# Four-bit weight codes unpacked in six vector operations instead of ten, and other orders of the sums and of two layer norms, in a macaron transformer block

## The chip, the cores and the metric

The kernel runs on one core of a Trainium2 chip. A core has a matrix engine (TensorE, "PE" in the profile; its weight loads are "PEld"), a vector engine (VectorE, "DVE"), a scalar engine (ScalarE, "ACT"), a general engine (GpSimd, "POOL") and an engine that here only issues transfers (SyncE, "SP"). Each works through its own instructions in the order in which they were written, and waits on semaphores for the others. The metric is the time of one execution on the device in microseconds. An order of instructions is written out by hand in this kernel: what the Python code calls first is first in its engine's queue.

## What is computed

One sequence of 2048 tokens of 512 numbers goes through half a feed-forward step, attention, and half a feed-forward step:

```python
x = x + 0.5 * ffn(layernorm(x), ...)
x = x + attention(layernorm(x), w_qkv, b_qkv, w_out, b_out)     # 16 heads of 32, causal
x = x + 0.5 * ffn(layernorm(x), ...)                            # the same weights as in the first

def dequant(W_packed, scales):          # two 4-bit codes in an integer, low one first
    idx = stack([W_packed & 15, W_packed >> 4 & 15]).reshape(N, K)
    return LUT[idx] * scales per block of 32
    # LUT = 0, .5, 1, 1.5, 2, 3, 4, 6 and the same with a minus sign
def ffn(x, ...):                        # 512 -> 4096 -> 512
    gate, up = x @ Wg.T, x @ Wu.T
    return (gelu_tanh(gate) * up) @ Wd.T
```

Bit 3 of a code is the sign, bits 2 and 1 an exponent and bit 0 a fraction; the table is that of such a small floating-point number, whose exponent zero is subnormal (0 and 0.5).

## The kernel before

**Phases.** `ffn(1, ...)`, `attention(...)` and `ffn(2, ...)` follow each other (L1035 to L1043). The tokens stay in SBUF as 16 tiles of 128 (`xs`). Phase 1 unpacks the weights and stores them in DRAM (`kept`); phase 2 loads them from there, so unpacking happens in phase 1 alone.

**The feed-forward step.** The 4096 hidden units are taken in 8 groups `g` of two halves `h` of 256. Tokens are taken in two halves `tp` of 1024, each of two blocks `tb` of 512. A product of two 2x2 block matrices is made from seven block products instead of eight (the Winograd scheme), which needs sums of blocks: of weights (`Rows.steps`, on GpSimd, L273 to L276: s3, then the changed a21, then s2, then s4), of tokens (`token_sums`, on VectorE, L295 to L298: t3, the changed b12, t2, t4) and of the hidden values (L399 to L402). Tile names in the profile: `w` weights, `xT_f` normalized and transposed tokens, `xsum` token sums, `pg` and `pu` gate and up products in PSUM.

`slot` (L320) makes the gate and then the up products of one half and one `tp`. The products' numbers run in the order 1, 2, 6, 7, 5, 4, 3. Number 1 is copied from PSUM by ScalarE into `u2` (L354), number 5 into `u4` (L366); the others are added by VectorE as they come (L357, L360, L363, L368, L372, L375), with one sum on GpSimd (L369). A gelu on ScalarE (L335) and a product on VectorE (L339) follow. Product 6 is the first that needs s2 and t2; 7 needs s3 and t3, 5 the changed blocks, and 3 and 4 s4 and t4. PSUM has seven buffers for all of these products and for transposes, taken in turn, so a product waits for the reading of the one seven before it.

After each product `slot` runs `rate` steps of a list `background` (the unpacking and the sums of weights needed later), one group of steps of layer norms in the first slots (`early` and `late`), and one step each of two more lists. The first slots of a phase are (h=0, tp=0), (h=1, tp=0), (h=0, tp=1), (h=1, tp=1) for the first group. The down projection follows each pair of slots (`down_pieces`).

**Unpacking.** `dequant_steps` (L212) works on 128 partitions by 512 words. Ten VectorE operations: shift and mask the magnitudes of both codes into two fp16 halves of a word (L233 to L235), bring the signs into place (L236, L237), turn the magnitude into its value by a multiplication, an addition and a minimum in fp16 (L239, L240), put the sign in (L241), and multiply by the scales once per code (L229, twice). They use three tiles: the codes `pk` (two buffers), `mag` and `val`. The codes and scales are loaded on SP's queue by `load_codes`. Phase 1 does this 48 times: 16 for gate, 16 for up, 16 for down weights.

**Layer norms.** `Norm` gives steps for a block of four tiles: moments (VectorE, `bn_stats` and `bn_aggr`, L112 and L113, or on ScalarE with `moments_on_act`), scales (a root on ScalarE and a reciprocal on VectorE, or with `power=True` a power on GpSimd, L124), a normalization of each tile (ScalarE if its number is in `on_act`, L142, otherwise VectorE, L144), and a transpose of each on TensorE with a copy from PSUM by ScalarE (L150, L151). The method `tiles()` gives n0, n1, t0, n2, t1, n3, t2, t3 (n for normalization, t for transpose).

At the start of phase 1 (L496 to L500) the norms of blocks 0 and 1 are written out ahead of the first slot, together with the unpacking of the first gate and up weights:

```python
n0 = Norm("f1", 0, xT[0], normed)
n1 = Norm("f1", 1, xT[1], normed, on_act=(0, 1), power=True)
gate, up = rows.steps(0), rows.steps(1)
run(n0.steps() + n1.moments + [n1.scales] + gate[:5] + n1.tiles() + gate[5:])
run(token_sums(0) + up)
```

Blocks 2 and 3 are normalized inside the first two slots: moments (ScalarE) and scales (GpSimd) in the first, normalizations and transposes in the second.

**The end of attention.** Heads go in pairs `p`, 0 to 7. For the last pair, `attend` takes two chunks of keys at a time; there are 40 chunks, 24 to 39 for the last 512 queries, of which 30 to 33 lie on the diagonal. For each such pair of chunks TensorE makes scores (L835, L844), ScalarE exponentials (L867), and TensorE the values of an earlier chunk (L774). After each chunk `n`, the steps that `extra` holds for `n` are run; among them is phase 2's first norm, of blocks 0 and 1 (L953 to L959): ten steps each, for block 0 one per chunk from 26 on, for block 1 two per chunk from 33 on. After the chunks come the last divisions (L810 and L813) and output projections (L659, added by VectorE in L662). Then phase 2 begins with `token_sums(0)`.

## Time and profile before

| what | us |
|---|---|
| median of the three runs shown | 3284.56 (3282.46 to 3284.75) |
| profiled execution, its own time | 3284.09 |
| span from first to last instruction in it | 3282.3 |
| TensorE busy (matmuls) | 3239.4 (99%) |
| VectorE busy | 2027.8 (62%) |
| GpSimd busy | 1145.8 (35%) |
| ScalarE busy | 875.7 (27%) |
| first feed-forward product starts | 21.21 |
| phase 2's first product starts | 2113.60 |

The profile is one execution taken by the hardware's profiler. A line of the time-ordered view gives start, duration, engine, source line, operation, what is written from what, and how many instructions were merged; in brackets stands how long the engine had been idle before it and what ended that idle time ("issue": nothing that the profile shows). Matmuls overlap, so a row of them is longer than the distance to the next by the end of the last one. The row of tenths shows the busy share in 40 slices of 82 us. In a table by stretches, each engine's busy time stands with its number of instructions, then the granted TensorE clock, the share of the transfer engines and GB/s.

### The profile page before, as it was taken

The page shows a single profiled execution, that of the slowest core. Times are in us where ns is not written, and L with a number is a line of the kernel's source. Part 1 is how long each engine was busy: PE and PEld are TensorE (multiplying, and loading weights), DVE is VectorE, ACT ScalarE, POOL GpSimd, SP SyncE. Part 2 cuts the span into 40 slices and gives each one's busy share as a digit, 9 for nine tenths or more (in the row PEclk, how much of TensorE's full clock was granted, in tenths as well). Part 3 has the DMA queues.
Part 4 walks back from the last instruction along what each step waited for, and adds up shares of the span by engine and source line. Part 5 has one row for each costly group of instructions (what it writes and reads, how often), then busy time and mean ns, then how long its engine had stood idle before and what let it go on. Part 6 is the DMA issues. An engine that isn't in the chain of part 4 may idle for free.

```text
span 3282.3 us, 34191 instructions
## 1 busy us (share of the span) xinstructions
PE 3239.4 (99%) x12656; PEld 1721.3 (52%) x12656; DVE 2027.8 (62%) x3110; ACT 875.7 (27%) x1849; POOL 1145.8 (35%) x1340
## 2 busy tenths in 40 slices
PE   6999999999999999999999999999999999999999
PEld 3556565655656565333344333356556565655556
DVE  7777777777777655565654675554455455445545
ACT  4111111111111131454543556431111111111111
POOL 3456464645646440332212223113122222313222
PEclk9999999999999999999999999999999999999999
DMA  3111111111111100000000000101010101101101
GB/s 137 47 66 66 68 42 71 65 45 67 67 68 42 74 17 7 6 15 6 13 5 6 30 20 9 49 23 45 23 55 36 45 23 45 37 31 45 45 23 52
DMA packets 42055, 134.15 MB, mean 41 GB/s; under 512 B 5864, under 2 KB 26344, under 8 KB 35360
## 3 DMA queue, kind: packets, MB, share of 16 engines
q1 hardware_dynamic: 41888, 131.96, 11.0%
q8 instruction: 100, 1.64, 0.2%
q14 instruction: 67, 0.55, 0.1%
HBM read 81.91 MB, written 48.46 MB: 40 GB/s over the span
## 4 chain that ended last, share of the span: by engine, by line
PE 94%; ACT 2%; DVE 2%; issue 1%; POOL 1%; DMA 0%; SPq 0%; POOLq 0%; DVEq 0%; ACTq 0%
PE po L414 23%; PE pu L315 23%; PE pg L315 23%; PE av L774 8%; PE pm L709 6%; PE pqk L620 4%; PE ps L835 2%; PE pv L637 2%; PE pp L659 2%; PE ps L844 1%; ACT pt L867 1%; PE pt_f L150 0%; ACT both L783 0%; PE pt_a L150 0%; POOL attnT L813 0%
## 5 line engine op out<-in xcount | busy, mean ns | idle before, releaser
L414 PE MATMUL po<-wd,inter 128*128 128x256 f32 x2048 | 482.2, 379 | 0.0
L315 PE MATMUL pg<-xT_f,w 128*128 128x512 f32 x1024 | 475.9, 592 | 2.2 <-DVE w L229 1.5
L315 PE MATMUL pu<-xT_f,w 128*128 128x512 f32 x1024 | 476.1, 592 | 1.3 <-DVE c L368 1.3
L414 PEld LDWEIGHTS po<-wd,inter 128*128 128x128 f32 x2048 | 389.0, 190 | 155.2 <-issue 106.0
L724 DVE TENSOR_REDUCE parts<-pm 128x1 f32<-128x512 f32 (+3 forms) x640 | 370.6, 608 | 149.6 <-PE pm L709 135.5
L369 POOL TENSOR_TENSOR u<-u,u 128x512 f32<-128x512 f32 x128 | 163.4, 1277 | 846.2 <-ACT u L366 846.2
L428 POOL TENSOR_TENSOR x<-x,d 128x512 f32<-128x512 f32 x248 | 333.3, 1355 | 343.6 <-DVE x L422 173.2
L315 PE MATMUL pg<-xsum,w 128*128 128x512 f32 x768 | 359.3, 597 | 3.9 <-issue 2.0
L414 PE MATMUL po<-wd,s 128*128 128x256 f32 x1536 | 362.4, 379 | 0.0
L315 PE MATMUL pu<-xsum,w 128*128 128x512 f32 x768 | 355.4, 592 | 0.4 <-DVE u L372 0.4
L414 PEld LDWEIGHTS po<-wd,s 128*128 128x128 f32 x1536 | 291.4, 190 | 116.2 <-issue 79.6
L709 PE MATMUL pm<-kT,qT 32*128 32x512 f32 (+3 forms) x1280 | 334.2, 574 | 0.1
L867 ACT ACTIVATE pt<-ps 128x512 f32<-128x512 f32 (+3 forms) x576 | 271.7, 532 | 132.8 <-PE ps L844 131.4
L774 PE MATMUL av<-pt,vaug 128*64 128x512 f32 (+3 forms) x1280 | 300.0, 553 | 2.8 <-ACT both L783 2.3
L315 PEld LDWEIGHTS pg<-xT_f,w 128*128 128x128 f32 x1024 | 194.3, 190 | 195.1 <-issue 179.5
L315 PEld LDWEIGHTS pu<-xT_f,w 128*128 128x128 f32 x1024 | 194.2, 190 | 193.4 <-issue 180.8
L844 PE MATMUL ps<-qT,kT 32*128 32x512 f32 (+3 forms) x1280 | 278.9, 536 | 0.0
L315 PEld LDWEIGHTS pg<-xsum,w 128*128 128x128 f32 x768 | 146.4, 192 | 148.1 <-issue 136.9
L315 PEld LDWEIGHTS pu<-xsum,w 128*128 128x128 f32 x768 | 145.7, 190 | 145.1 <-issue 136.8
L422 DVE SCALAR_TENSOR_TENSOR x<-po,x 128x512 f32<-128x512 f32 x192 | 131.5, 685 | 112.8 <-ACT d L436 83.2
L861 POOL TENSOR_SCALAR_AFFINE_SELECT pt<-pt 128x256 f32<-128x256 f32 x128 | 52.3, 408 | 395.9 <-ACT pt L860 394.7
L422 DVE SCALAR_TENSOR_TENSOR d<-po,d 128x512 f32<-128x512 f32 x192 | 131.8, 686 | 82.1 <-PE po L414 81.2
(140 smaller groups left out, 3606.2 us busy)
## 6 DMA issues: line engine op xcount, KB each, us to landing
kept<-wd SPq DMA_DIRECT2D x8, 1792.0 KB
wd<-kept SPq DMA_DIRECT2D x8, 1792.0 KB
x<-in_x SPq DMA_DIRECT2D x16, 256.0 KB
pk<-in_gate_codes SPq DMA_DIRECT2D x16, 256.0 KB
sc<-in_gate_scales SPq DMA_DIRECT2D x32, 128.0 KB
pk<-in_up_codes SPq DMA_DIRECT2D x16, 256.0 KB
sc<-in_up_scales SPq DMA_DIRECT2D x32, 128.0 KB
pk<-in_down_codes SPq DMA_DIRECT2D x16, 256.0 KB
```

The source lines that it names most:

```text
L315: nc.tensor.matmul(ps, lhsT=a[:, j, :], rhs=b[:, j, :], start=(j == 0), stop=(j == 1))
L369: nc.gpsimd.tensor_tensor(u4, u4, u2, ALU.add)
L414: nc.tensor.matmul(ps[:, j, :], lhsT=a[i][:, k, bass.ts(2 * q + j, P)], rhs=b[i][:, k, :], start=(k == 0), stop=(k == 1),)
L422: stt(dst, ps, 0.5, other, ALU.mult, ALU.add)
L428: adder.tensor_tensor(dst, dst, other, ALU.add)
L620: nc.tensor.matmul(ps, lhsT=w[:, j, k, :], rhs=xT[tb][:, k, :], start=(k == 0), stop=(k == 3))
L637: nc.tensor.matmul(ps[:, i, :], lhsT=xT[t // 4][:, k, (t % 4) * P : (t % 4 + 1) * P], rhs=wv_sb[:, k, bass.ts(half, 256)], start=(k == 0), ...
L709: nc.tensor.matmul(ps[a][:, :n], lhsT=q[r, bass.ts(4 * g + i, P)], rhs=k[r, kb * 512 : kb * 512 + n], start=True, stop=not on_pe,)
L724: nc.vector.tensor_reduce(parts[:, a, i, kb : kb + 1], ps[a][:, :n], AX.X, ALU.max)
L774: nc.tensor.matmul(av[64 * a : 64 * a + 64, off:], lhsT=vaug[:, c, p % 4, HD * a : HD * a + 2 * HD], rhs=pt[:, a, off:], start=(c == 0), s ...
L844: nc.tensor.matmul(ps[a][:, off:], lhsT=k[r, bass.ts(c, P)], rhs=q[r, g * 512 + off : (g + 1) * 512], start=False, stop=True,)
L867: nc.scalar.activation(pt[:, a, plain:], ps[a][:, plain:], AF.Exp, scale=scale)
```

## The change

Six things are changed.

- The unpacking takes six operations: the signs and both codes are brought into the two halves of a word in place, the three magnitude bits are shifted to bits 9 to 11 of each half, and sign and magnitude are joined. Such a half, read as fp16, has the code's exponent as its two lowest exponent bits and the code's fraction as its highest fraction bit; it is the code's value divided by 16384, and subnormal for 0.5. The scaling multiplies by 16384 instead of 0.25. The result lies in the codes' tile itself, so `val` is gone and `pk` is held until the second scaling.
- The weights' sums: s2 is made second, as a22 - s3, ahead of the changed a21.
- The token sums: t2 is made second, as t3 + b11, ahead of the changed b12. In phase 2, for the first half of the tokens, t3 is made on GpSimd.
- The tile `u2` has two buffers instead of one.
- The first norms: block 1 takes its scales by a root on ScalarE and a reciprocal on VectorE, its tiles 0 and 1 are normalized on GpSimd and 2 and 3 on VectorE, into tiles of their own tags (`u3`, `c11`), and are transposed in the order 2, 0, 3, 1. Two operations of the unpacking come ahead of block 1's scales and four after its normalizations.
- The last pair's norm of block 1: its ten steps come after chunks 32, 33, 34, 35, 36, 36, 37, 37, 38, 39 instead of two per chunk from 33 to 37.

```diff
+        def __init__(
+            self, phase, tb, t_out, temp, on_act=(0, 1, 2, 3), on_pool=(), moments_on_act=False, power=False
+        ):
...
-                    nc.vector.tensor_scalar(xn[i], tiles[i], mv[:, i, 0:1], rstd[:, i : i + 1], ALU.subtract, ALU.mult)
+                    eng = nc.gpsimd if i in on_pool else nc.vector
+                    eng.tensor_scalar(xn[i], tiles[i], mv[:, i, 0:1], rstd[:, i : i + 1], ALU.subtract, ALU.mult)
...
-                val = dq.tile([P, 512, 2], F16, tag="val", name=f"val_{nm}")
+                val = pk.bitcast(F16).rearrange("p (n b) -> p n b", b=2)
...
-                    stt(o, v, 0.25, s, ALU.mult, ALU.mult)
+                    stt(o, v, 16384.0, s, ALU.mult, ALU.mult)
...
-                    lambda: tsc(mag, w, 9, 0x0E00, ALU.logical_shift_left, ALU.bitwise_and),
-                    lambda: stt(mag, w, 21, mag, ALU.logical_shift_left, ALU.bitwise_or),
-                    lambda: tsc(mag, mag, 0x0E000E00, 0x40004000, ALU.bitwise_and, ALU.bitwise_or),
-                    lambda: tsc(v32, w, 12, 0x8000, ALU.logical_shift_left, ALU.bitwise_and),
-                    lambda: stt(w, w, 24, v32, ALU.logical_shift_left, ALU.bitwise_or),
-
-                    lambda: tsc(v16, f16, 2.0, -4.0, ALU.mult, ALU.add),
-                    lambda: nc.vector.tensor_tensor(v16, f16, v16, ALU.min),
-                    lambda: stt(v32, w, 0x80008000, v32, ALU.bitwise_and, ALU.bitwise_or),
+                    lambda: tsc(mag, w, 12, 0xF000, ALU.logical_shift_left, ALU.bitwise_and),
+                    lambda: stt(w, w, 24, mag, ALU.logical_shift_left, ALU.bitwise_or),
+                    lambda: tsc(mag, w, 3, 0x0E000E00, ALU.logical_shift_right, ALU.bitwise_and),
+                    lambda: stt(w, w, 0x80008000, mag, ALU.bitwise_and, ALU.bitwise_or),
                     lambda: scaled(0),
                     lambda: scaled(1),
...
                         lambda: eng.tensor_tensor(s3, a11, a21, ALU.subtract),
+                        lambda: eng.tensor_tensor(s2, a22, s3, ALU.subtract),
                         lambda: eng.tensor_tensor(a21, a21, a22, ALU.add),
-                        lambda: eng.tensor_tensor(s2, a21, a11, ALU.subtract),
...
+                first = nc.gpsimd if phase == 2 and tp == 0 else eng
...
-                    lambda: eng.tensor_tensor(t3, b22, b12, ALU.subtract),
+                    lambda: first.tensor_tensor(t3, b22, b12, ALU.subtract),
+                    lambda: eng.tensor_tensor(t2, t3, b11, ALU.add),
                     lambda: eng.tensor_tensor(b12, b12, b11, ALU.subtract),
-                    lambda: eng.tensor_tensor(t2, b22, b12, ALU.subtract),
...
-                            u2 = temp("u2", 1)
+                            u2 = temp("u2")
...
+                tags = ["u3", "u3", "c11", "c11"]
                 n0 = Norm("f1", 0, xT[0], normed)
-                n1 = Norm("f1", 1, xT[1], normed, on_act=(0, 1), power=True)
+                n1 = Norm(
+                    "f1", 1, xT[1], lambda nm: ap.tile([P, D], F32, tag=tags.pop(), name=nm, bufs=2),
+                    on_act=(), on_pool=(0, 1),
+                )
                 gate, up = rows.steps(0), rows.steps(1)
-                run(n0.steps() + n1.moments + [n1.scales] + gate[:5] + n1.tiles() + gate[5:])
+                tiles = n0.tiles()
+                run(n0.moments + [n0.scales] + n1.moments + tiles[:6] + gate[:2] + [n1.scales] + tiles[6:])
+                run([n1.normal[i] for i in (0, 2, 1, 3)] + [n1.transposed[i] for i in (2, 0, 3, 1)] + gate[2:])
...
-                            extra.setdefault(STARTS[3] + (2 + i if tb == 0 else 9 + i // 2), []).append(step)
+                            after = 2 + i if tb == 0 else (8, 9, 10, 11, 12, 12, 13, 13, 14, 15)[i]
+                            extra.setdefault(STARTS[3] + after, []).append(step)
```

More of the change, by code (lines that the diff above doesn't have):

```diff
@@ L78, in macaron_kernel @@
     class Norm:
-        def __init__(self, phase, tb, t_out, temp, on_act=(0, 1, 2, 3), moments_on_act=False, power=False):
+        def __init__(
+            self, phase, tb, t_out, temp, on_act=(0, 1, 2, 3), on_pool=(), moments_on_act=False, power=False
+        ):
             nm = f"{phase}_{tb}"
@@ L216, in dequant_steps @@
                 mag = dq.tile([P, 512], U32, tag="mag", name=f"mag_{nm}")
-                val = dq.tile([P, 512, 2], F16, tag="val", name=f"val_{nm}")
-                f16 = mag.bitcast(F16)
-                v16 = val.rearrange("p n b -> p (n b)")
-                v32 = v16.bitcast(U32)
+                val = pk.bitcast(F16).rearrange("p (n b) -> p n b", b=2)
                 tsc, stt = nc.vector.tensor_scalar, nc.vector.scalar_tensor_tensor
```

## The prediction

> **What bounds the kernel.** I read the page's busy times and slices first, then the chain that ended last, TensorE's waits, a table by stretches cut where those waits lie, and the instructions in order of time around them.
>
> ```profile
> PE 3239.4 (99%) x12656; PEld 1721.3 (52%) x12656; DVE 2027.8 (62%) x3110; ACT 875.7 (27%) x1849; POOL 1145.8 (35%) x1340
> PE   6999999999999999999999999999999999999999
> ...
> PE 94%; ACT 2%; DVE 2%; issue 1%; POOL 1%; DMA 0%; SPq 0%; POOLq 0%; DVEq 0%; ACTq 0%
> ```
>
> TensorE is busy everywhere but in the first slice (82 us). The change removes no matmul, so it can gain only where TensorE waits. Columns of the next table: stretch, its length, then busy us of PE, PEld, DVE, ACT, POOL, granted clock.
>
> ```profile
> 0.00:21.21 21.21, 7.99 (x33) 6.10 (x33) 12.79 (x30) 10.72 (x17) 3.40 (x12) 1.00 0.79 247
> 21.21:50.57 29.36, 25.07 (x56) 10.27 (x56) 24.41 (x34) 13.59 (x35) 15.82 (x16) 1.00 0.32 117
> 50.57:78.08 27.51, 20.33 (x53) 10.06 (x54) 18.77 (x30) 13.11 (x25) 8.47 (x10) 0.75 0.22 86
> 78.08:91.35 13.27, 13.23 (x39) 6.19 (x38) 10.40 (x15) 4.66 (x8) 1.53 (x1) 1.00 0.11 40
> ```
>
> A product of two 256-deep matmuls takes 1.72 us (28 instructions in 12.02 us), 14 products a slot, 24.0 us. The first slot takes 29.36. The gate half of the second (12.0 plus six tiles' transposes at 0.5) takes 27.5, partly at half clock. After 78.08 nothing is lost until the last head pair. The places:
>
> ```profile
> 20.37 1.29 DVE L229 SCALAR_TENSOR_TENSOR w<-val,sc 128x512 f32<-128x512 f16 x2
> 21.21 3.67 PE L315 MATMUL pg<-xT_f,w 128*128 128x512 f32 x8 [1.51 <-DVE w L229]
> ...
> 26.77 3.70 PE L315 MATMUL pg<-xsum,w 128*128 128x512 f32 x8 [1.89 <-POOL w L275]
> ...
> 56.80 0.59 ACT L354 COPY u<-pg 128x512 f32<-128x512 f32 x1 [2.98 <-POOL u L369]
> 58.15 1.13 PE L150 MATMUL pt_f<-ident,xn_f 128*128 128x128 f32 x4 [3.88 <-ACT xn_f L142]
> 65.42 1.13 PE L150 MATMUL pt_f<-ident,xn_f 128*128 128x128 f32 x4 [2.72 <-ACT xn_f L142]
> ...
> 2090.75 0.72 PE L150 MATMUL pt_f<-ident,xn_f 128*128 128x128 f32 x4 [2.82 <-DVE xn_f L144]
> 2119.18 3.67 PE L315 MATMUL pg<-xsum,w 128*128 128x512 f32 x8 [1.98 <-issue]
> ```
>
> The first weights are ready at 21; the third product waits for a sum on GpSimd; the second slot waits for normalized tiles; the last pair does too; phase 2's third product waits for its token sum (L297 ends 2119.07, hence "issue" at 2119.18).
>
> **The skill.** "VectorE: DVE Perf Modes", the tier table, has a one-input operation in SBUF at twice the rate of a two-input one; the trace agrees: 0.42 us (L235) against 0.69 (L234). "SBUF — State Buffer", Who interferes with whom: VectorE's two-input and two-port operations contend with GpSimd; the same token sum takes 1.22 us alone and 1.63 beside GpSimd. "TensorE: Matmul & The Clock Gate", Part 1: an idle window of about 3.4 us halves the clock, and Part 4 says that transposes don't count as work. Here the clock is 0.50 from 58 to 70 us after the 3.88 us wait, and 0.50 from 2091.4 to 2094.6 after the 2.82.
>
> **The change, part by part.**
>
> *Start of phase 1.* VectorE's order to 11.85 us (moments of both norms) stays. Then come two unpacking operations (0.43 + 0.73, start to start), done at 13.0. The second norm's root now goes to ScalarE behind the fourth normalization (ends 13.34): 0.30 (no table load lies between the first root and the normalizations), reciprocal 0.18, so scales at 13.85. Before, the power on GpSimd was done at 14.88 and VectorE stood still from 14.5 to 17.15. Two tiles on VectorE at 0.55 end at 14.95, or 15.5 if GpSimd holds the port. GpSimd's one-input pass over 512 elements has no row: affine_select on 256 took 0.41, a two-input sum on 512 1.27; I take 0.9 each (range 0.65 to 1.3), done at about 15.7, or 16.5 at worst. TensorE has four tiles from 14.5, done by 17; ScalarE's copies end about 17.6. VectorE's remaining four operations: 15.5 + 0.43 + 0.73 + 2 x 0.63 = 17.9, the first half of the weights at 17.3. **First product 17.4 instead of 21.21.**
>
> GpSimd now makes s3, then s2: two sums (1.1 and 1.6, partly contended) from 17.9, done 20.6, not third in line (26.71 before). VectorE's token sums start at 17.7; t2 is second, 17.7 + 2 x 1.6 = 20.9. The third product wants to start at 17.4 + 3.67 = 21.1: **no wait, 21.1 instead of 26.77.** The up half then starts at 21.1 + 5 x 1.72 = 29.7 (was 35.45). Its weights: token sums end 24.0, six operations 0.43 + 0.72 + 0.43 + 0.72 + 2 x 0.63 = 3.6, ready at 27.6, against 34.15 before.
>
> *First two slots.* Everything ScalarE and VectorE do next hangs on that 27.6. Before, the next evacuation (L357) started 1.4 us after 34.15, and ScalarE's gelu, sums, squares and copy ran to 43.0; moved 6.5 us they end at 36.5. TensorE's twelfth product then waits about 0.5 for a bank (before: 1.30 and 0.39), and the second slot's first product waits 1.2 for the copy behind the second set of sums (43.6): **slot two at 43.65 instead of 50.57.** The squares end at 46.4, two copies at 47.5. The second of these (L354) waited until 56.80 for GpSimd because its tile had one buffer; with two it doesn't. Normalization 0.82: first transpose at 48.4 after a wait of 1.3 (was 3.88). The next needs ScalarE past the gelu of c11, which waits for VectorE: L369 on GpSimd ends at 49.6 behind the norm's scales; two VectorE operations and one unpacking (1.7) bring 51.3; c11, gelu, normalization 0.7 + 0.6 + 0.8: 53.45, a wait of 2.85 (was 2.72). I take the clock as staying full, since the idle time between products is 1.8 and 3.35 us, not the 4.8 of before. From 53.45: 4 products, 5 tiles at 0.47 and a wait of 0.6 give **the up half at 63.3 instead of 78.08: 14.8 us.** From there the trace has no wait, and I add none.
>
> *Other unpackings.* Four operations fewer in each of 46 more calls, in effect those of L234, L235, L239 and L240. From 92 to 1160 us these are busy 47.2 + 20.9 + 44.7 + 35.9 = 148.7 us in 43 calls, 3.5 a call. All of it is covered by TensorE: group 3's gate weights are scaled by 424.2 and first used at 452.55, its up weights by 448.9 and 476.65, 28 us of cover. Without cover each call would be worth 3.5. The codes' buffer is now held to the second scaling, 5 us longer at 419 to 424; the next load on SP is behind a scales' load that waits for this anyway, and its data are used at 454.
>
> *Last pair's norm.* Its first moments move one step ahead, under VectorE's wait for the transpose (idle 3.91 us before 2084.83); the transposes move to the next two pairs of chunks. From 2087.93 TensorE goes on with scores. Gone are 2.82, 0.25, and half of the 3.2 us at half clock, 1.6: **4.7 us.** Two tiles' copies come later, but before the copy that the divisions hang on, so that chain moves as a whole.
>
> *Phase 2's token sums.* The first goes to GpSimd behind L813 (ends 2112.58): 1024 elements at the slope of 0.72 (256) and 1.27 (512) are 2.4, done 2115.0, as VectorE comes free (2115.34); t2 is then first there and ends at 2116.6, before the third product (2117.2). **2.0 us.** If contended to 4 us, 1.0 would be left.
>
> Sum: 14.8 + 4.7 + 2.0 = 21.5. Span 3282.3 - 21.5 = 3260.8; the profiled execution took 3284.09, 1.8 more than its span, and lies within 0.5 of the median: **3262.6 us.**
>
> **Rivals.** (a) The waits of 1.3 and 2.85 in slot two still halve the clock: 3 to 5 us given back, about 3267; for it, 2.82 was enough in the last pair. 0.18. (b) The last pair gains nothing, as scores wait for banks that ScalarE frees (it has 2 us of exponentials per pair): 3267. 0.10; with (a), 3270 to 3272, 0.04. (c) VectorE runs so far ahead that slot two's waits go too, 5.9 us more: 3257. 0.11. (d) Slower: the scaling reads subnormal fp16, an operand that no row shows. It takes 0.63 alone and up to 1.36 on average. The same skill page, Specifications, says that VectorE computes in fp32, where these numbers are normal, so I take no extra cost; the lower bound is none too, as the other 4 bytes are the same. It makes VectorE the bound only if each takes some 4.8 us more: from 92 to 1160 us VectorE is idle 262 us (1068.0 less 806.0 busy), the removed operations give 149, shared by 86 scalings: (262 + 149) / 86 = 4.8. 0.05. (e) No measurable change, the waits having merely moved: 0.02.
>
> **Numbers.** The forecast as worked has 0.50 (own range 3260 to 3266). 3256.5 to 3271 takes in (a), (b), (c) and the bounds of GpSimd's passes. Slower than 0.2% (6.6 us, about what a measurement can tell) is (d); faster is the rest, 0.93.
>
> **What would show it.** Right: first product near 17.4, third without a wait on GpSimd, slot two near 43.7, its up half near 63, no wait of L150 near 2087, and none before phase 2's third product. Wrong: half clock between 45 and 60 us, GpSimd's normalization above 1.3 us, or new waits after 92 us.

## The result, and the profile after

The changed kernel takes 3267.42 us (median of four, 3266.87 to 3267.80), where the kernel before, measured beside it, takes 3283.51: a ratio of 0.9951, 95% interval 0.9934 to 0.9968. That is 16.1 us gained where 21.5 were forecast. The profiled execution took 3267.61 us, 1.8 more than its span of 3265.8, as before.

The profile of one execution is shown here, as for the kernel before. The busy times and slices of its page, in the columns of before:

```profile
PE 3236.0 (99%) x12656; PEld 1720.2 (53%) x12656; DVE 1887.5 (58%) x2918; ACT 873.4 (27%) x1848; POOL 1130.4 (35%) x1339
PE   7999999999999999999999999999999999999999
```

VectorE lost 140 us of work, and TensorE's time is what it was: the first slice alone looks different, 7 tenths instead of 6. The table by stretches, cut at the same four events (first product, slot two, its up half, 13.27 us of undisturbed work after it):

```profile
0.00:19.86 19.86, 8.09 (x32) 6.26 (x33) 11.55 (x27) 8.79 (x15) 7.14 (x12) 1.00 0.88 279
19.86:46.43 26.57, 26.17 (x57) 11.17 (x56) 20.86 (x29) 14.21 (x36) 14.46 (x17) 1.00 0.35 121
46.43:68.48 22.05, 17.43 (x52) 8.74 (x53) 14.14 (x22) 12.89 (x25) 6.20 (x8) 0.92 0.27 106
68.48:81.75 13.27, 13.23 (x38) 6.20 (x37) 9.87 (x15) 4.65 (x8) 1.80 (x1) 1.00 0.10 35
```

The first stretch is 1.35 us shorter than before, the second 2.8, the third 5.5 (22.05 beside 27.51), and the fourth is the same 13.27. The instructions in order of time that answer to those shown of before:

```profile
13.34 1.37 DVE L147 TENSOR_SCALAR xn_f<-x,mv_f,rstd_f 128x512 f32<-128x512 f32 x2
13.41 5.47 POOL L147 TENSOR_SCALAR xn_f<-x,mv_f,rstd_f 128x512 f32<-128x512 f32 x2 [12.04 <-DMA sc<-in_up_scales]
15.81 1.29 DVE L229 SCALAR_TENSOR_TENSOR w<-pk,sc 128x512 f32<-128x512 f16 x2
18.94 1.12 PE L153 MATMUL pt_f<-ident,xn_f 128*128 128x128 f32 x4 [1.14 <-POOL xn_f L147]
19.86 5.57 PE L313 MATMUL pg<-xT_f,w 128*128 128x512 f32 x8
25.27 3.60 PE L313 MATMUL pg<-xsum,w 128*128 128x512 f32 x8
...
46.43 3.70 PE L313 MATMUL pg<-xT_f,w 128*128 128x512 f32 x8 [0.40 <-ACT u L352]
50.93 0.74 PE L153 MATMUL pt_f<-ident,xn_f 128*128 128x128 f32 x4 [0.79 <-ACT xn_f L144]
56.64 0.75 PE L153 MATMUL pt_f<-ident,xn_f 128*128 128x128 f32 x4 [3.25 <-ACT xn_f L144]
57.22 2.88 PE L313 MATMUL pg<-xsum,w 128*128 128x512 f32 x4
...
2098.41 2.36 POOL L293 TENSOR_TENSOR xsum<-xT_f 128x1024 f32<-128x1024 f32 x1
2099.34 3.60 PE L313 MATMUL pg<-xT_f,w 128*128 128x512 f32 x8
2102.78 3.60 PE L313 MATMUL pg<-xsum,w 128*128 128x512 f32 x8
```

The weights are scaled by 17.1, but the last tile comes from GpSimd at 18.9, so the first product starts at 19.86. It and the start of the second run at about half rate (the row of both, eight instructions, takes 5.57 us instead of 3.7). The third product has lost its wait for GpSimd. Slot two still waits twice for normalized tiles, and the longer wait is followed by four instructions in 2.88 us instead of 1.88, at a granted clock of 0.50 from 58 to 61 us. At the end of attention no wait for a tile is left, and phase 2's third product follows the second without a gap.

| place | before | forecast | after |
|---|---|---|---|
| first product | 21.21 | 17.4 | 19.86 |
| phase 1's up half | 35.45 | 29.7 | 33.85 |
| slot two | 50.57 | 43.65 | 46.43 |
| slot two's up half | 78.08 | 63.3 | 68.48 |
| gained there | | 14.8 | 9.6 |
| gained by the last pair | | 4.7 | 4.5 |
| gained by phase 2's token sums | | 2.0 | 2.1 |

The last two rows: scores at one and the same place start at 2081.75 before and 2072.02 after (9.73 earlier), phase 2's first product at 2113.60 and 2099.34 (14.26, so 4.5 more), its third at 2119.18 and 2102.78 (16.4, so 2.1 more). What is missing is all in the first 70 us.

Two things limit how finely single profiles can be read there. The third token tile's statistics begin at 6.28 us before and at 5.85 after, and from 5.34 to 6.83 in the profiles below, ahead of anything that an edit touches, so a place can differ by up to 1.5 us without a cause in the edit; 0.43 of the 9.6 gained at the up half are of this kind. And the profile taken for GpSimd's operations below is of this same kernel up to its last microseconds. In it the first transposes start 0.1 us earlier than in the profile above, the first product at 19.20 and slot two at 45.77, and the second tile is waited for just as long:

```profile
55.98 0.75 PE L153 MATMUL pt_f<-ident,xn_f 128*128 128x128 f32 x4 [3.25 <-ACT xn_f L144]
56.57 1.88 PE L313 MATMUL pg<-xsum,w 128*128 128x512 f32 x4
```

The four instructions behind that wait take 1.88 us here, at a granted clock of 1.00, and the up half starts at 66.17, which is 11.9 us earlier than before instead of 9.6. From the second tile's transpose to the up half it is 10.19 us here and 11.84 above: the half clock cost 1.65 us in one execution of this kernel and nothing in another.

### The profile page after: what moved, and what is told of

The parts are those of the page before. It is cut to its first block, busy times and chain, and to the rows that moved or that the text cites. A ratio compares the mean times of both kernels' runs of the same rounds, so it can differ in the third digit from the quotient of the medians.

```text
span 3265.8 us, 34006 instructions
## 1 busy us (share of the span) xinstructions
PE 3236.0 (99%) x12656; PEld 1720.2 (53%) x12656; DVE 1887.5 (58%) x2918; ACT 873.4 (27%) x1848; POOL 1130.4 (35%) x1339
## 4 chain that ended last, share of the span: by engine, by line
PE 95%; ACT 2%; DVE 1%; POOL 1%; issue 1%; DMA 0%; SPq 0%; POOLq 0%; DVEq 0%; ACTq 0%
PE po L412 24%; PE pu L313 23%; PE pg L313 23%; PE av L779 8%; PE pm L714 6%; PE pqk L625 4%; PE ps L840 2%; PE pv L642 2%; PE pp L664 2%; PE ps L849 1%; ACT pt L872 1%; PE pt_f L153 0%; ACT both L788 0%; DVE parts L729 0%; PE pt_a L153 0%
## 5 line engine op out<-in xcount | busy, mean ns | idle before, releaser
L426 POOL TENSOR_TENSOR x<-x,d 128x512 f32<-128x512 f32 x248 | 323.5, 1315 | 333.2 <-DVE d L420 164.8
```

The source lines that it names most:

```text
L426: adder.tensor_tensor(dst, dst, other, ALU.add)
```

## The experiments

**What was to be told apart.** My theory after the result: the loss is the price of one operation, GpSimd's normalization, which I had guessed at 0.9 us and which took 5.47 for two; without it the start would be as forecast and so would the rest. The rival: the start's gain is lost again in slot two whatever the start does, since something behind it (ScalarE's moments, VectorE's evacuations, the clock) sets its own pace there. Beside that, each part of the change was to get its own price. In all fences below the lines are those of the view in order of time, unless said otherwise.

### Block 1 normalized on VectorE alone

```diff
-                    on_act=(), on_pool=(0, 1),
+                    on_act=(), on_pool=(),
```

> The changed kernel with block 1's tiles 0 and 1 normalized on VectorE instead of GpSimd (about 0.55 us each instead of 3.13 and 2.35). Theory G: GpSimd's two passes, done at 18.9 us, hold the start; then the last transpose comes near 17, the first product near 17.3 instead of 19.86, and the kernel is 2.5 to 4 us faster than the changed one. Rival H: the start is set by ScalarE's copies and the half-rate TensorE; then less than 1 us is gained.

Measured 3266.33 us (3266.18 to 3267.36; ratio to before 0.9950, 0.9935 to 0.9965), so 1.1 less than the changed kernel by the medians, or 0.5 more gained when each is set against the kernel before as measured beside it (16.6 beside 16.1), with intervals that overlap. 2.5 to 4 were expected.

```profile
17.76 3.72 PE L313 MATMUL pg<-xT_f,w 128*128 128x512 f32 x8
22.03 3.67 PE L313 MATMUL pg<-xsum,w 128*128 128x512 f32 x8 [0.55 <-DVE xsum L294]
45.04 3.70 PE L313 MATMUL pg<-xT_f,w 128*128 128x512 f32 x8 [1.67 <-ACT u L352]
55.25 1.01 PE L153 MATMUL pt_f<-ident,xn_f 128*128 128x128 f32 x4 [3.25 <-ACT xn_f L144]
```

The first product is where the forecast had it (17.76 for 17.4), the third comes 3.2 us earlier than in the changed kernel (22.03 for 25.27). Four normalizations on VectorE take 1.91 us in all. But of the 3.2 us only 1.4 are left at slot two: its first product now waits 1.67 instead of 0.40, for ScalarE's copy. The two waits there are the same 0.79 and 3.25, again with half clock behind the second. So both theories hold a part: the price at the start is real, and slot two takes more than half of it back. Even with VectorE alone, slot two is 1.4 us later than forecast (45.04 for 43.65): block 1's transposes end at 18 instead of 17, and the token sums and the third product follow some 0.9 us late.

### GpSimd's operations measured by themselves

The kernel is the changed one, with instructions on scratch added at its very end; 512 and 256 elements, three of each kind. VectorE's last sums run until 3260.66, so the first two passes are beside them, and all the others are alone.

```diff
+    for n in (512, 256):
...
+            nc.gpsimd.tensor_scalar(pc[:, :n], pa[:, :n], pb[:, 0:1], pb[:, 1:2], ALU.subtract, ALU.mult)
...
+            nc.gpsimd.tensor_scalar(pc[:, :n], pa[:, :n], 2.0, 3.0, ALU.subtract, ALU.mult)
...
+            nc.gpsimd.tensor_scalar(pc[:, :n], pa[:, :n], pb[:, 0:1], None, ALU.subtract)
...
+            nc.gpsimd.tensor_tensor(pc[:, :n], pa[:, :n], pb[:, :n], ALU.subtract)
```

> The changed kernel with GpSimd instructions on a scratch tile appended at its end, when the other engines are done: tensor_scalar on 512 and 256 numbers with two per-partition scalars, with two constants, with one per-partition scalar, and tensor_tensor. If the form with per-partition scalars is dear in itself, it takes 2.2 to 2.5 us for 512 alone, against 0.6 to 1.3 with constants; if the 2.35 and 3.13 us at the start came from sharing the port with VectorE, it takes below 1.3 alone. It says nothing on the total time, which grows by the appended work.

The time was 3293.86 us, which holds the added work. First the third instruction of the normalization's kind (two scalars per partition), which is alone, then groups by line and shape, with busy us and mean ns of one after the bar: two constants, one scalar, two tensors.

```profile
3261.29 2.07 POOL L1056 TENSOR_SCALAR probe<-probe 128x512 f32<-128x512 f32 x1
```

```profile
L1058 POOL TENSOR_SCALAR probe<-probe 128x512 f32<-128x512 f32 x2 | 3.8, 1922 | 0.2
L1060 POOL TENSOR_SCALAR probe<-probe 128x512 f32<-128x512 f32 x3 | 4.7, 1561 | 0.3
L1062 POOL TENSOR_TENSOR probe<-probe 128x512 f32<-128x512 f32 x3 | 3.8, 1262 | 0.2
```

The expectation had two branches and missed with both: alone the pass is below 2.2 us, and two constants cost nearly as much as two scalars per partition, so it isn't these scalars that make it dear. The normalization's pass costs 2.07 us alone, 3.8 times VectorE's 0.55 and 1.6 times a two-input sum on the same engine. "GPSIMD Engine Reference", 4.1 Engine selection, calls one-input work there roughly line-rate and two-input work about twice as slow as on VectorE. The second agrees (1.26 against 0.69); the first does not hold for this operation, and the measurement decides. Beside VectorE, at the start, the two passes took 2.35 and 3.13 us (2.34 and 2.57 in this second profile): up to 1.06 more than alone. The probe shows more of this by chance. Beside its second pass VectorE made two two-input sums, and the pass took 3.10 us; beside its first VectorE made one, the pass took 2.09, and the sum 1.06 instead of 0.69. So either side can be the one that is held up.

### Ten operations in the changed kernel

The old unpacking with its `val` tile, and `u2` with one buffer, since both don't fit.

```diff
-                    stt(o, v, 16384.0, s, ALU.mult, ALU.mult)
+                    stt(o, v, 0.25, s, ALU.mult, ALU.mult)
...
+                    lambda: tsc(v16, f16, 2.0, -4.0, ALU.mult, ALU.add),
+                    lambda: nc.vector.tensor_tensor(v16, f16, v16, ALU.min),
...
-                            u2 = temp("u2")
+                            u2 = temp("u2", 1)
```

> The changed kernel with the ten old unpacking operations, and u2 with one buffer (the third tile needs its space; the run u2_one separates that). If the unpacking carries the gain at the start: the first gate weights are still hidden behind GpSimd's normalization, but the first up weights come 2.2 us later, and slot one's evacuations lag again; the second slot's up half moves from 68.5 to 72 to 77 us, 4 to 8 us slower than the changed kernel. Rival: the other orders carry it, and this run is within 2 us of u2_one.

### One buffer for u2 in the changed kernel

```diff
-                            u2 = temp("u2")
+                            u2 = temp("u2", 1)
```

> The changed kernel with one buffer for u2. The second slot's first copy on ScalarE waits again for GpSimd's sum (ends near 52.4 us), so the first tile's transpose comes at 53.9 instead of 50.9; the next one, at 56.6, does not move. If that is all, nothing is lost; but TensorE then stands without a product from 50 to 54.3 us, so the half clock comes earlier and lasts longer: 1 to 3 us slower than the changed kernel. Rival: no difference beyond 0.5 us.

Ten operations: 3275.48 us (3274.80 to 3277.67; ratio 0.9977, 0.9968 to 0.9986). One buffer: 3266.58 us (3265.22 to 3270.90; ratio 0.9952, 0.9937 to 0.9967), no different from two buffers at 3267.42. So the shorter unpacking is worth 8.9 us between these two, which were measured side by side. First ten operations, then one buffer:

```profile
42.99 1.96 PE L321 MATMUL pu<-xT_f,w 128*128 128x512 f32 x4 [1.34 <-DVE c L374]
57.54 1.13 PE L153 MATMUL pt_f<-ident,xn_f 128*128 128x128 f32 x4 [3.88 <-ACT xn_f L144]
65.29 0.75 PE L153 MATMUL pt_f<-ident,xn_f 128*128 128x128 f32 x4 [3.21 <-ACT xn_f L144]
```

```profile
53.02 0.75 PE L153 MATMUL pt_f<-ident,xn_f 128*128 128x128 f32 x4 [3.65 <-ACT xn_f L144]
53.60 1.88 PE L313 MATMUL pg<-xsum,w 128*128 128x512 f32 x4
55.87 0.75 PE L153 MATMUL pt_f<-ident,xn_f 128*128 128x128 f32 x4 [0.39 <-ACT xn_f L144]
```

With ten operations the products wait for VectorE's evacuations again (1.34), both long waits of slot two are back, and its up half starts at 77.16, about 1 us before the 78.08 of the kernel before: without the shorter unpacking the new order at the start brings next to nothing. With one buffer the first tile is late (3.65) and the second is not (0.39); with two it is the other way round, 0.79 and 3.25. The second buffer moves the wait from one tile to the next. With one, the first tile's normalization stands behind a copy that waits 2.75 us for GpSimd's sum; the second one's stands behind a gelu that waits for VectorE either way, and ScalarE reaches it at 55.02 with one buffer and at 55.78 with two. No half clock follows the 3.65 here, and the up half starts at 66.06, as in the second profile of the changed kernel (66.17).

### The end of attention undone

```diff
-                first = nc.gpsimd if phase == 2 and tp == 0 else eng
+                first = eng
...
-                            after = 2 + i if tb == 0 else (8, 9, 10, 11, 12, 12, 13, 13, 14, 15)[i]
+                            after = 2 + i if tb == 0 else 9 + i // 2
```

> The changed kernel with the old places of the last pair's norm steps and with phase 2's first token sum on VectorE (t2 still second). From the last pair's wait at the 1.9 us (2072.0 in the changed kernel) to phase 2's first product: 27.3 us in the changed kernel, 31.9 here, with half clock again. The third product of phase 2 then waits about 0.5 us for t2 rather than 2.0, since the order alone brings most of that gain. Rival: the last pair's gain came from the earlier moments or from elsewhere and the distance stays below 29 us.

One run: 3274.34 us, 6.9 more than the changed kernel's median; it gains 8.6 on the kernel before as measured beside it, where the changed kernel gains 16.1.

```profile
2080.79 1.10 PE L153 MATMUL pt_f<-ident,xn_f 128*128 128x128 f32 x4 [2.82 <-DVE xn_f L147]
2109.39 3.67 PE L313 MATMUL pg<-xsum,w 128*128 128x512 f32 x8 [0.42 <-PE pg L313]
```

The wait of 2.82 is back to the hundredth, and the half clock with it. From the scores at 2072 to phase 2's third product this kernel is 6.6 us later than the changed one (2109.39 beside 2102.78, from starts that lie within 0.3). Some 1.7 of that are more than in the kernel before, since the stretch at half clock lasted longer: eight products of values took 3.54 us in it, where before they took 2.50. Of the wait before that product only 0.42 of 1.98 is back, as the order of the sums (t2 second) is still the new one: the order brings 1.6, and GpSimd's t3 the last 0.4.

### The six operations alone, in the kernel before

```diff
-                    lambda: tsc(v16, f16, 2.0, -4.0, ALU.mult, ALU.add),
...
+                    lambda: stt(w, w, 0x80008000, mag, ALU.bitwise_and, ALU.bitwise_or),
```

> The kernel before with the six-operation unpacking and nothing else. If the unpacking carries the start's gain, phase 2's first product comes 7 to 9 us earlier than before and the time is near 3275; if it needs the other orders (the third product waiting for the third sum on GpSimd, the norm's power on GpSimd), the gain is below 4 us, above 3279. The last pair's wait of 2.8 us and the half clock stay in both.

3277.09 us (3272.62 to 3279.30 in nine runs; ratio 0.9975, 0.9965 to 0.9985): 6.4 us gained.

```profile
24.95 5.37 PE L307 MATMUL pg<-xsum,w 128*128 128x512 f32 x8 [2.32 <-DVE xsum L289]
2073.86 3.25 PE L766 MATMUL av<-pt,vaug 128*64 128x512 f32 x8
2112.11 3.67 PE L307 MATMUL pg<-xsum,w 128*128 128x512 f32 x8 [1.99 <-issue]
```

The first product starts at 19.02, earlier than in the changed kernel, and slot two's up half at 69.00, 9.1 us earlier than before. That is nearly the whole 9.6 that the changed kernel gains there, with GpSimd's pass, the orders of the sums and the second buffer absent. The waits of the end are all there (1.99). Not all of the 9.1 lasts: 8.6 are left at the last pair's scores (2073.16 for 2081.75), and right behind these eight products of values take 3.25 us instead of 1.72, at a granted clock of 0.50, after a wait of 1.88 that the kernel before has too. That is why the profiled run has 7.1 of it at phase 2's third product, and its time, the median of the nine, 6.4.

### The old orders of the sums

The kernel with block 1 on VectorE, and s2 and t2 back in their old places; t3 stays on GpSimd in phase 2.

```diff
-                        lambda: eng.tensor_tensor(s2, a22, s3, ALU.subtract),
...
+                        lambda: eng.tensor_tensor(s2, a21, a11, ALU.subtract),
...
-                    lambda: eng.tensor_tensor(t2, t3, b11, ALU.add),
...
+                    lambda: eng.tensor_tensor(t2, b22, b12, ALU.subtract),
```

> The run norm_vector with the old order of the weights' and the tokens' sums (the changed blocks second, s2 and t2 third from them). In phase 1 the third product waits for t2 as third token sum: it starts 1.2 to 1.7 us later than the 22.03 of norm_vector; but slot two's first product hardly moves, as it waits for ScalarE by 1.67 us in norm_vector. In phase 2, where t3 stays on GpSimd, t2 is second on VectorE and the third product waits about 0.5 us. In all 0 to 2 us slower than norm_vector. Rival: the order of sums carries 3 us or more, as the forecast's arithmetic for the third product has it (26.77 to 21.1).

One run: 3269.52 us. The third product waits 1.96 for t2 and then runs slowly:

```profile
23.67 5.37 PE L313 MATMUL pg<-xsum,w 128*128 128x512 f32 x8 [1.96 <-DVE xsum L295]
```

Yet slot two's up half starts at 67.21, against 67.11 with the new orders (counted from each profile's first transposes it is no later either). In phase 1 the orders of the sums remove a visible wait and no time: slot two absorbs it. The 3.2 us that this run has over the kernel with the new orders come later: by 0.8 before the last pair's scores at 2071, by 1.6 right behind them, where eight products of values take 3.22 us instead of 1.72, and by 0.9 at phase 2's third product, which waits 0.73. Only the last has to do with the edit. The slow products are the clock: 0.51 is granted there, and 1.00 over the same products with the new orders. The wait ahead of them is 1.88 or 1.89 us in all thirteen profiles of this document; four of them have the clock at 0.50 to 0.57 behind it (this one, the six operations alone, and the two kernels with spread moments below), the other nine don't. Kernels with either order are on both sides, so it doesn't follow the orders. The 0.8 stays unexplained.

### The moments of block 3, then of both blocks, moved to VectorE

In the kernel with block 1 on VectorE, phase 1's moments of block 3, and in a second kernel those of block 2 too, are made by VectorE. This tests the reading of the 1.67 above, that ScalarE's moments hold slot two.

```diff
-                Norm(f"f{phase}", tb, xT[tb], normed, moments_on_act=True, power=True) for tb in (2, 3)
+                Norm(f"f{phase}", tb, xT[tb], normed, moments_on_act=phase == 2 or tb == 2, power=True) for tb in (2, 3)
```

> The run norm_vector with the moments of the fourth block in phase 1 taken on VectorE (four times 0.66 + 0.18 us) instead of ScalarE (eight passes, 5.7 us with their readings). Theory A: what is still lost in slot two is set by ScalarE, whose sums and squares stand ahead of the copies and the gelu; then slot two starts without its 1.67 us wait, near 43.4 us, the 3.25 us wait for the second tile shrinks below 1, no half clock follows, and slot two's up half comes at 60 to 63 instead of 67.1: 4 to 7 us faster than norm_vector. Rival V: VectorE's own evacuations set it, and 3.4 us more on VectorE make it slower.

> As vector_moments, with the third block's moments on VectorE too. If ScalarE was the bound, the first evacuations no longer wait for it at 37 us either (2.94 us idle on VectorE there), and it is as fast as vector_moments or up to 1 us faster; if VectorE is the bound by now, it is 1 to 3 us slower than vector_moments.

3268.01 us (3267.70 to 3268.86; ratio 0.9950, 0.9936 to 0.9965) and 3268.07 (3267.98 to 3269.15; 0.9950, 0.9934 to 0.9967): no gain over the kernel with block 1 on VectorE, rather about 1 us less (15.5 and 15.4 gained on the kernel before as measured beside them, where that one gains 16.6). In the first of them:

```profile
55.37 0.63 ACT L333 ACTIVATE c<-c 128x512 f32<-128x512 f32 x1 [8.42 <-DVE c L355]
56.76 1.13 PE L153 MATMUL pt_f<-ident,xn_f 128*128 128x128 f32 x4 [5.61 <-ACT xn_f L144]
```

Slot two starts 1.4 us earlier, at 43.68, and without a wait for ScalarE. Then ScalarE stands idle for 8.42 us until VectorE, which now has the moments too, has evacuated the product that the gelu needs; the normalization is queued behind that gelu, and the wait grows from 3.25 to 5.61. That reading fell: with less on ScalarE and more on VectorE the wait grows, so it isn't the moments' amount on ScalarE that makes the long wait, but VectorE's evacuations.

### The moments spread earlier, and a normalization put ahead of the gelu

What makes VectorE late? Its instructions in the changed kernel, and ScalarE's gelu behind them:

```profile
38.54 0.69 DVE L366 TENSOR_TENSOR c<-pg,u 128x512 f32<-128x512 f32 x1 [2.94 <-ACT u L364]
46.41 0.69 DVE L355 TENSOR_TENSOR c<-pu,u 128x512 f32<-128x512 f32 x1 [1.47 <-ACT u L352]
54.53 0.68 DVE L355 TENSOR_TENSOR c<-pg,u 128x512 f32<-128x512 f32 x1
55.25 0.63 ACT L333 ACTIVATE c<-c 128x512 f32<-128x512 f32 x1 [4.38 <-DVE c L355]
55.78 0.80 ACT L144 ACTIVATE xn_f<-x,nbias_f,rstd_f 128x512 f32<-128x512 f32 x1
```

VectorE stands still 2.94 and 1.47 us for copies that ScalarE makes behind whole groups of moments (four squares, four sums, some 3 us each), and then works without a pause of more than 0.5 us to 54.53, late by that. The gelu waits for it, and the normalization for the gelu. So the two engines seem to hold each other up in turn. Two kernels test it, both with block 1 on VectorE. The first starts ScalarE's moments sooner and spreads them over other products; the second also puts the second normalization of slot two one step earlier, ahead of the gelu.

```diff
+            if phase == 1:
+                early = [n2.moments, [], [n3.moments[0]], [], [n3.moments[1]], [n2.scales], [], [n3.scales]]
```

> The run norm_vector with phase 1's ScalarE moments placed earlier, none moved to another engine: block 2's right behind the first product's copy (ScalarE stood idle there 8.7 us), block 3's behind products 3 and 5. Theory I, the two engines hold each other up: VectorE's evacuations stood idle 2.94 and 1.47 us for ScalarE's copies and are then late in slot two. Without these idles the second slot starts without its 1.67 us wait, near 43.4, the first evacuation of slot two (53.14 in norm_vector) comes near 48.7, the wait for the second tile falls from 3.25 to about 1.8, no half clock follows, and the up half comes near 61.3 instead of 67.1: 5 to 6 us faster than norm_vector. Rival V, VectorE's own work is the bound: the idles go but it is late all the same, and less than 2 us is gained.

```diff
+            if phase == 1:
+                late[0].append(late[1].pop(0))
```

> As moments_early, and in phase 1 the second tile's normalization stands behind the first one's, ahead of the gelu that waits for VectorE. Then the second tile's transpose no longer waits for VectorE, and the up half of slot two comes at 58.5 to 60.5: 1 to 3 us faster than moments_early. If another wait takes its place (the third tile's normalization stands behind the same gelu), below 1 us.

The first: 3263.30 us (3260.49 to 3264.16; ratio 0.9939, 0.9924 to 0.9954). The second: **3259.66 us** (3258.81 to 3260.99; ratio 0.9929, 0.9912 to 0.9945), and the fastest of all. Against the kernel before as measured beside each, the first gains 19.4 us and the second 23.0, where the changed kernel gains 16.1 and the one with block 1 on VectorE 16.6. First the one, then the other:

```profile
45.24 0.63 PE L153 MATMUL pt_f<-ident,xn_f 128*128 128x128 f32 x4
48.88 0.68 DVE L355 TENSOR_TENSOR c<-pg,u 128x512 f32<-128x512 f32 x1
50.99 1.13 PE L153 MATMUL pt_f<-ident,xn_f 128*128 128x128 f32 x4 [3.40 <-ACT xn_f L144]
51.91 3.03 PE L313 MATMUL pg<-xsum,w 128*128 128x512 f32 x4
```

```profile
48.22 0.63 PE L153 MATMUL pt_f<-ident,xn_f 128*128 128x128 f32 x4
49.84 0.63 ACT L333 ACTIVATE c<-c 128x512 f32<-128x512 f32 x1 [3.27 <-DVE c L355]
51.71 0.75 PE L153 MATMUL pt_f<-ident,xn_f 128*128 128x128 f32 x4 [1.14 <-ACT xn_f L144]
```

With the moments spread, slot two starts at 41.80 without a wait, and VectorE's two pauses before it are gone. But 3.0 us are gained where 5 to 6 were expected, for the wait for the second tile is still there (3.40, half clock behind it). The first tile's transpose comes at 45.24 instead of 49.54 and the evacuation that the gelu needs at 48.88 instead of 53.14: TensorE and VectorE are both 4.3 us earlier, so the distance between them, which makes the wait, stays. From 28.28 to 51.10 VectorE is now busy for 22.1 of 22.8 us; what stands ahead of that evacuation is its own work. The up half starts at 62.66, for 67.11 with block 1 on VectorE. With the normalization ahead of the gelu that transpose follows at once (48.22); the gelu still waits 3.27 for VectorE, but what is queued behind it is now the third tile, and TensorE waits 1.14 for that, with no half clock. The up half starts at 59.70, 8.8 us before the changed kernel's. So two things are shown. ScalarE's moments in front of copies that VectorE needs held back the start of slot two, TensorE and VectorE alike, and not the wait inside it. And VectorE's lateness reached TensorE through the gelu in front of the normalization. How short the wait would be with less work in VectorE's queue ahead of that evacuation, no run tests.

## Why the prediction was right in sign and too large

**GpSimd's pass: a mis-sized term.** "I take 0.9 each (range 0.65 to 1.3)" is the step that failed first, and one of the prediction's own signs of being wrong: 2.07 alone, 2.35 and 3.13 where it stood. I had set a one-input operation below the two-input sum of 1.27, by the nearest row and its size; on GpSimd it is dearer. The last tile came at 18.9 instead of 15.7, the first product at 19.86 instead of 17.4. With those two tiles on VectorE it came at 17.76, so the other terms of that chain (unpacking ahead of the scales, the root on ScalarE, four operations instead of eight behind) come out within 0.4 in sum; none of them was measured by itself. Behind it the forecast was somewhat short: it starts the token sums at 17.7, though its own sum has VectorE busy to 17.9, and with VectorE alone they start at 18.62 and the third product at 22.03 instead of 21.1.

**Half rate at the start: not in the forecast.** The third product starts 5.41 us after the first (19.86 to 25.27), where the forecast had 3.67. This and the 2.46 above make the up half 4.15 late. In the second profile of the same kernel it starts 4.09 us after the first, and the up half, at 31.95, is 2.25 late. Slot two is only 2.8 late, since the waits of 0.5 and 1.2 that I had put before it were 0 and 0.40.

**Slot two's waits: right in sum, wrong in what follows.** I had 1.3, 2.85 and 0.6 and measured 0.79, 3.25 and 0.58: 4.75 against 4.62. What failed in this profile is "I take the clock as staying full": the granted clock was 0.50 from 58 to 61, and from the second transpose to the up half it took 11.84 us instead of 9.85. That is rival (a), at 2.0 us and not at 3 to 5, and another of the prediction's signs of being wrong, half clock between 45 and 60 us. The stretch before the second transpose was 0.4 longer than forecast. Together 2.8 + 2.0 + 0.4 = 5.2, the whole of the 14.8 - 9.6. In the second profile the clock did stay full behind the same 3.25, and 2.1 us are missing at slot two, 0.4 before the second transpose and 0.3 behind it, 2.9 in all. So the reason that the prediction gave for a full clock, a shorter idle time than before, decides nothing here, and whether its assumption holds was a matter of chance. The measured 3267.42 meets rival (a)'s 3267, outside the forecast's own range of 3260 to 3266 and inside the wide one; but the half clock has at most 2.0 of what is missing and in one profile none, the rest being GpSimd's pass, the start at half rate and some small terms. That the number of rival (a) was met is luck.

**u2's second buffer: the wait moved.** The forecast let the 3.88 turn into 1.3, and 0.79 is what came, as the buffer's effect. But with one buffer the other wait is 0.39 instead of 3.25, which I had not seen: the copy that waits for GpSimd's sum then holds back the first tile, and by the time the second is due the gelu ahead of it has its input nearly ready. The whole step is worth nothing that these runs can tell.

**The orders of the sums in phase 1.** The third product lost its wait as forecast. That it would carry through to slot two's up half is wrong by the one run that tests it: 67.21 and 67.11.

**Last pair and phase 2's sums.** 4.5 and 2.1 us, forecast 4.7 and 2.0. GpSimd's sum over 1024 elements took 2.36 (I had 2.4), and every wait named there is gone.

**Unpacking elsewhere, and subnormal operands.** From 90 to 1160 us VectorE's busy time fell from 808.0 to 674.3 us, and TensorE had no wait there before or after: all covered, as forecast. The scalings of gate and up weights took 975 ns on average after and 1283 before, those of the down weights 822 both times, and 674 to 678 ns at the least both times. So scaling subnormal fp16 numbers costs nothing extra here, and rival (d) fell by the trace. Rivals (b) and (e) fell with the last pair's 4.5 us and with the result; rival (c), waits that vanish in slot two, needed two more edits.

**Which part brought what.** The six operations alone bring 6.4 us, with the rest of the change around them 8.9; the end of attention 6.6 by the traces of before and after (4.5 + 2.1). The one run without it has 6.9, which is no clean price: 1.7 of it is half clock that the kernel before didn't have, and it still has the order of the sums, worth 1.6. The 8.9 and the 6.6 sum to 15.5 of the 16.1. GpSimd's normalization costs some 0.5 to 1.1 by the times and 1.4 at slot two in the profiles (0.7 by the second one), which is little above what these can tell; the second buffer and phase 1's orders bring nothing measurable. The new route of block 1's scales and the order of its unpacking were not measured by themselves.

## What to carry to other kernels

Don't price an operation from another kind of operation on the same engine: where the profile has no row for it, a forecast's range has to reach well above the nearest row, and moving a tile to an "idle" engine can put it on the path that sets the end. A wait that hangs on what stands in front in an engine's queue doesn't go away with an earlier start or a second buffer; here it stayed as it was or moved to another tile, until the gelu that stood ahead of the normalization was put behind it. Moments ahead of a copy held back the stretch as a whole, which is a gain of another kind: ask whether an edit moves the waiting engine and the awaited one alike. Read for each late instruction what is queued ahead of it on its own engine, not only what its semaphore names. And a profile is one execution: two of the same kernel lay 2.3 us apart at the same place here (66.17 and 68.48), so give a half clock to an edit only when a second profile has it too.

## What the runs showed of the hardware that was not expected

- GpSimd's `tensor_scalar` on 128x512 fp32 takes 2.07 us with two scalars per partition, 1.92 with two constants, 1.56 with one scalar and one operation; `tensor_tensor` takes 1.26. Beside VectorE the first takes 2.34 to 3.13.
- A wait's length alone didn't decide whether the clock halved. The same kernel, behind the same 3.25 us, had 0.50 granted in one profile and 1.00 in another; 3.40 was followed by half clock with the moments spread, 3.65 with one `u2` buffer by a full one. Behind the 1.88 us before the last pair's scores it fell to 0.50 to 0.57 in four of thirteen profiles. "TensorE: Matmul & The Clock Gate", Part 1, has the activity windows run freely, not from the start of a wait; these runs agree with that, and don't prove it. The 3.4 us that the prediction took from there is no bound for a single wait as the profile shows it; whether the transposes and short products around a wait count as idle too, no run here shows.
- The granted clock doesn't show every slow stretch. In the changed kernel the weight loads of the first products came 0.85 us apart and then 0.43, with a recorded clock of 1.00 throughout:

```profile
22.42 0.33 PEld L313 LDWEIGHTS pg<-xT_f,w 128*128 128x128 f32 x1 [0.52 <-issue]
23.27 0.33 PEld L313 LDWEIGHTS pg<-xT_f,w 128*128 128x128 f32 x1 [0.52 <-issue]
23.98 0.19 PEld L313 LDWEIGHTS pg<-xT_f,w 128*128 128x128 f32 x1 [0.38 <-issue]
24.41 0.19 PEld L313 LDWEIGHTS pg<-xT_f,w 128*128 128x128 f32 x1 [0.24 <-issue]
```

The first eight instructions of the products took 5.57 and 4.12 us in the two profiles of the changed kernel, 3.72 with block 1 on VectorE and 6.10 with ten operations. So it differs from one execution to the next, and single profiles can't lay it to an edit. Why the rate is halved there stays open; that the array hadn't yet reached full clock after a start of transposes and pauses is an argument, and no run tests it.
